# Zeros of a scratch tensor laid by two stages: three channels behind each image's store in attention, two behind each step's store in the scans

## The chip, the cores and the metric

One Trainium2 chip, one core. The metric is the device time of one execution of the whole program in microseconds (us), as the median of several runs. Profiles show one execution each. Engines: PE does matrix products (PEld its weight loads), DVE and ACT elementwise work, POOL (GpSimd) as well, and SP here only issues transfers (DMA).

## The reference

The input x is [32 images, 192 channels, 56, 56] in float32. Four layers follow, each with a group normalisation and a residual:

```
x = x + agent_attention(groupnorm(x))       # layer 0: 6 heads, 49 agents, depthwise 3x3 convolution, projection
x = x + bidirectional_wkv(groupnorm(x))     # layer 1: k, v, r by matrices; scans forwards and backwards over 3136 pixels; layernorm; Wo
x = x + shift_and_blur(groupnorm(x))        # layer 2: each channel shifted by its own offset with zeros beyond the edge, then a 3x3 kernel
x = x + long_convolution(groupnorm(x))      # layer 3: 55x55 filter per channel, by FFT
```

Layers 0 and 1 mix channels within an image. Layers 2 and 3 work on one channel over all images. Layer 2 reads zeros where the shift reaches beyond the image, and that is what the zeros of this change are for.

## The kernel before

The program has four parts in a row: a filter (about the first 190 us), `attention` (layer 0), `scan_pairs` (layer 1), and `channel_blocks` (layers 2 and 3). Between them the data goes through tensors in device memory: `x1` after layer 0, `x2` after layer 1.

**x2 and its gaps.** `x2` is laid out by channel, then half of the images, then row, then image, then column. Rows have a pitch of 112 floats: 56 of data (`x2`) and 56 of zeros (`gaps`). `channel_blocks` reads each channel at an offset in this flat space, so a column beyond the edge reads zeros. The zeros of a channel are one transfer from a small tile `zeros` in on-chip memory: 2 x 57 x 16 pieces of 56 floats (1824 pieces of 224 bytes, 399 KB). There are 192 such transfers, one for each channel; I call one a lay. They write other bytes than the data, and nobody reads them before `channel_blocks`.

**attention.** A loop over 32 images `b`. Two images are in on-chip memory at a time (a pool with two buffers), so the load of image b+2 (L392, L394, in `_Ready.image`) waits for the store of image b (L863, L865). Within an image, four column blocks `j` are worked on:

- `weigh`, `gather` and others on PE, with ACT and DVE between them;
- `convolve`: eight steps on DVE for each of two tiles (L619), the first tap on ACT (L617), from `v_a` and `v_c` that ACT copies out in `find_v` (L593, L604);
- `moments` of the next image: DVE's `bn_stats` on the first tile (L485, seven) and on the second (L487, four), the first use of the loaded image;
- `ask`, `answer`, `project`, and the store.

After each image's store the lays of some channels are issued on SP (L870), six or seven after each of images 0 to 27 and none after the last four. A dependency without a semaphore (`NoSync`) keeps them behind the last store in SP's order.

**scan_pairs.** 16 pairs of images in four chunks of 784 pixels each. It begins by loading weights and constants (L937, L942, L943) and the sums that attention left (L1064, L1066). Then come four `forwards` of the first pair, and a loop of 64 steps. A step interleaves three passes, each of which loads its own three tiles of `x1` (L1019, four transfers on SP):

- `backwards` of a chunk: ACT normalises x (L1111), PE multiplies by Wr (L891, L894, L901, L904 in the helper `_Pairs`), ACT makes the gate g (L1189, L1193, L1194), DVE scans backwards (L1129, L1131), ACT inverts the denominator (L1136, L1137), DVE combines (L1197, L1198, L1199);
- `finish` of the chunk before: PE centres y (weights `fixed`), ACT squares it (L1214), PE takes the mean of the squares, ACT takes the inverse root (L1223, L1224), PE multiplies y by `wog`, DVE scales (L1237) and adds x (L1240), and four stores to `x2` leave on SP (L1254);
- `forwards` of a chunk of the next pair: ACT L1111, PE with Wk and Wv, ACT exp (L1160, `ek`), DVE the product (L1165, `bv`), the scans, y (L1175).

There are seven buffers for the tiles of x, and a load takes three, so a load waits until an earlier pass has let go of its tiles. The last steps of finish are followed by three squares of the new x on ACT (L1247).

The order on each engine's queue is found by a scheduler when the program is built: it lists each engine's instructions by its own estimate of when they become ready. [...] SP's list holds loads, stores and lays together.

Of the kernel before, what the change touches and what calls it, by code (L numbers as in the profile page):

```python
# [28 lines left out]
C = 192  # L29
T = 96  # L30
S = 56
# [38 lines left out]
LEAD = 64  # L70
# [334 lines left out]


@with_exitstack
def attention(ctx: ExitStack, tc: tile.TileContext, a, ready, x1, st_a, st_c, x2, gaps):

# [6 lines left out]
    nc = tc.nc  # L418
    NB = x1.shape[0]
# [15 lines left out]
    n = C + 1  # L435
# [370 lines left out]
    for b in range(NB):  # L806
        x, more = nxt, b + 1 < NB
        if more:
            nxt = ready.image(nc, a, b + 1)
        low, sums = small("low", [PAIR, NK, 3]), small("sums", [PAIR, NK, 3])  # L810
        got = sp.tile([PAIR, NK, C], F32, name="got", tag="got", bufs=1)
        turned, asked, back = {}, {}, {}
        for j in range(NK):
            prs = weigh(j, gk, low, sums)
            if j == 0:
                gq = seen(ag, wqT, gq_c, "gq_a")
            vT = turn_v(j, v[j])
            if j > 0:
                halves = gather(j - 1, *turned[j - 1])
            if j + 2 < NK:  # L820
                v[j + 2] = find_v(j + 2)
            turned[j] = turn(j, prs), vT
            if j > 0:
                settle(j - 1, halves, got)
            if j + 1 < NK:
                o[j + 1] = convolve(j + 1)
            elif more:
                mv, pools = moments(nxt)
        halves = gather(NK - 1, *turned[NK - 1])
        asked[0] = ask(0, gq)  # L830
        settle(NK - 1, halves, got)
        values = join(low, sums, got)
        done, o = o, {}
        st = small("st", [128, 2, 9])
        for t in range(1, NK + 2):
            if t < NK:
                asked[t] = ask(t, gq)
            if more and t == 1:
                mean, d = spread_of(mv)
            if more and t == 2:  # L840
                rs, nb = scaling(mean, d, pools)
                normed(nxt, rs, nb, 0)
            if t <= NK:
                back[t - 1] = turn_back(t - 1, asked[t - 1])
            if more and t in (3, 4):
                v[t - 3] = find_v(t - 3)
            if t >= 2:
                project(t - 2, done[t - 2], x, st)
            if t <= NK:
                answer(t - 1, back[t - 1], values, done[t - 1])  # L850
            if more and t == 2:
                ag = find_agents(b + 1, pools)
                normed(nxt, rs, nb, 1)
            if more and t == 3:
                gk = seen(ag, wkT, gk_c, "gk_a")
                normed(nxt, rs, nb, 2)
            if more and t == 4:
                o[0] = convolve(0)
                normed(nxt, rs, nb, 3)
        nc.sync.dma_start(out=st_a[:, b % 2, b // 2], in_=st[:, 0])  # L860
        for h, r in HALVES:
            nc.sync.dma_start(out=st_c[b % 2, :, h, b // 2], in_=st[r, 1])
        nc.sync.dma_start(out=x1[b, 0:128], in_=x[0].rearrange("p y x -> p (y x)"))  # L863
        for h, r in HALVES:
            stored = nc.sync.dma_start(  # L865
                out=x1[b, 128:C, 1568 * h : 1568 * h + 1568], in_=x[1][r].rearrange("p y x -> p (y x)")
            )
        early = max(1, NB - 4)
        for c in range(C * min(b, early) // early, C * min(b + 1, early) // early):
            laid = nc.sync.dma_start(  # L870
                out=gaps[c].rearrange("s h g w -> (s h) g w"),
                in_=zeros[:, 0:S].unsqueeze(1).to_broadcast([2 * (S + 1), NB // 2, S]),
            )
            behind = mybir.DependencyInfo(mybir.DependencyClass.NoSync, mybir.DependencyReason.DATA)
            tc.add_manual_dep(laid.ins, stored.ins.name, behind, reason="no burst")


class _Pairs:
# [26 lines left out]


@with_exitstack
def scan_pairs(ctx: ExitStack, tc: tile.TileContext, a, k, x1, st_a, st_c, x2, rs2, count):

# [11 lines left out]
    def small(name, shape):  # L923
        return cp.tile(shape, F32, name=name, tag=name)
# [69 lines left out]
    nc.vector.memset(eps, 4.0 * LN_EPS)  # L994
    kept_a, kept_c = small("kept_a", [128, 2, NB // 2]), small("kept_c", [128, NB // 2])
    fine = small("fine", [128, NB // 2])
    tops = small("tops", [128, 5, 3 * NM])
    for i, top in enumerate((1e8, 1e15, 1e15, 1e15, 1e30)):
        nc.vector.memset(tops[:, i], top)
# [202 lines left out]
    def finish(s, m):  # L1202

        h, xs = s.y[m], load(s.p, m)
        hs = [parts(t) for t in h]
        sq = [wp.tile([128, MC], F32, name="sq", tag="t") for _ in range(3)]
        for tiles in ((0, 1), (2,)):
            ps = [turned() for _ in tiles]
            if len(tiles) == 2:
                pairs.outer(centre, [q[2] for q in ps], hs)  # L1210
            else:
                pairs.inner(centre, ps[0][2], hs)
            for t, (_, both, _) in zip(tiles, ps):
                nc.scalar.activation(  # L1214
                    sq[t].rearrange("p (h n) -> p h n", h=2), both, AF.Square,
                    accum_out=s.seen[:, 4, 3 * m + t : 3 * m + t + 1],
                )
        sqs = [parts(t) for t in sq]
        pv = [turned() for _ in range(2)]
        pairs.outer(mean_w, [q[2] for q in pv], sqs)  # L1220
        rds = [wp.tile([128, MC], F32, name="rd", tag="t") for _ in range(3)]
        for t, (_, both, _) in enumerate(pv):
            nc.scalar.activation(rds[t].rearrange("p (h n) -> p h n", h=2), both, AF.Ln, bias=eps)  # L1223
            nc.scalar.activation(rds[t], rds[t], AF.Exp, scale=-0.5)  # L1224

        for t, r in enumerate((slice(0, 64), slice(64, 128))):
            nc.scalar.dma_start(out=rds[2][r], in_=rds[t][r])
        yield
        left = []
        for tiles in ((0, 1), (2,)):  # L1230
            po = [turned() for _ in tiles]
            if len(tiles) == 2:
                pairs.outer(wog, [q[2] for q in po], hs)
            else:
                pairs.inner(wog, po[0][2], hs)
            for t, (_, out, _) in zip(tiles, po):
                nc.vector.tensor_tensor(  # L1237
                    sq[t].rearrange("p (h n) -> p h n", h=2), out, rds[t].rearrange("p (h n) -> p h n", h=2), ALU.mult
                )
                nc.vector.scalar_tensor_tensor(  # L1240
                    xs[t], sq[t], cb[:, of(t)], xs[t], ALU.add, ALU.add, accum_out=s.sums[:, t, m : m + 1]
                )
                if m == NM - 1:
                    nc.vector.tensor_scalar(s.away[:, t], s.sums[:, t, m : m + 1], -1.0 / MC, None, ALU.mult)

                def square(t=t):
                    nc.scalar.activation(  # L1247
                        sq[t], xs[t], AF.Square, bias=s.away[:, t], accum_out=s.squares[:, t, m : m + 1]
                    )

                left.append(square)
        rows = slice(m * MC // S, (m + 1) * MC // S)
        for r, t, i, c in places:
            nc.sync.dma_start(out=x2[c, i, rows, s.p], in_=xs[t][r].rearrange("p (h w) -> p h w", w=S))  # L1254
        yield left

    def conclude(s):
# [546 lines left out]
def all_blocks(ctx: ExitStack, tc: tile.TileContext, a, k, out):  # L1804
# [10 lines left out]
    x2, gaps = wide[..., 0:S], wide[..., S:PITCH]  # L1815
    filt, rs2 = scratch("filt", [C, KS * KS]), scratch("rs2", [C, 2, NB // 2])
    spectra = scratch("spectra", [84, C, 2, 42])
    shifts = scratch("taps", [2 * (S + 1), C // 4, 9]), dp.tile([1, C // 4], I32, name="begins", tag="begins")
    st_a, st_c = scratch("st_a", [128, 2, NB // 2, 9]), scratch("st_c", [2, 64, 2, NB // 2, 9])
    with tc.tile_pool(name="a_r", bufs=1) as rp, tc.tile_pool(name="a_x", bufs=2) as xp:  # L1820
        ready = _Ready(rp, xp)
        make_filter(tc, a, k, filt, spectra, shifts, lambda: ready.load(nc, a, k))
        attention(tc, a, ready, x1, st_a, st_c, flat, gaps)
    with tc.tile_pool(name="count", bufs=1) as cp:
        count = cp.tile([1, 1], I32, name="count", tag="count")
        scan_pairs(tc, a, k, x1, st_a, st_c, x2, rs2, count)
        n = nc.values_load(count[0:1, 0:1], min_val=0, max_val=128)
        with tc.If(n > 0):
            scan_guarded(tc, a, k, x1, x2, rs2)
# [105 lines left out]
```

## Time and profile before

| | us |
|---|---|
| median of 3 runs | 12223.37 (12220.62 to 12237.54) |
| the profiled execution, its own time | 12221.27 |
| its span | 12219.5 |
| attention, about | 190 to 4985 |
| scans, about | 4985 to 8455 |
| channel blocks, about | 8455 to 12219 |
| PE busy | 11048.8 (90%) |
| DVE busy | 10766.9 (88%) |
| ACT busy | 7140.2 (58%) |
| POOL busy | 3332.8 (27%) |
| transfers in SP's queue | 840.69 MB, 30.1% of 16 DMA engines' span |

How to read it: the span is the time from the first to the last event of the profiled execution. "Busy" is an average over three long stages with different limits, so each stage has to be looked at by itself. Times within the profile are counted from the start of the span.

### The profile page before, as it was taken

Reading aid. Unit: us, or ns where it says so; the run is one execution under the profiler, and the core shown is the slowest. Engines: PE = TensorE matmul, PEld = TensorE weight load, DVE = VectorE, ACT = ScalarE, POOL = GpSimd, SP = SyncE. Lnnn points to the kernel's source line nnn. Section 1 sums busy time; section 2 is a strip of 40 time slices with the busy share of each in tenths; the row PEclk is TensorE's granted clock in tenths of the full one; section 3 lists DMA queues with packets and bytes.
Section 4 is the critical chain, followed back from the end, with each engine's and each line's share of the span. In section 5 each row is a group of like instructions: output and inputs, shape, how many; then the busy total and the mean of one; then the engine's idle time right before and its main releaser. Section 6 shows DMA issues by size and latency. Waiting matters only on the chain. (4 is left out here: it accounts for less than half of the span.)

```text
span 12219.5 us, 157479 instructions
## 1 busy us (share of the span) xinstructions
PE 11048.8 (90%) x57358; PEld 6621.1 (54%) x57358; DVE 10766.9 (88%) x14738; ACT 7140.2 (58%) x14684; POOL 3332.8 (27%) x2552
## 2 busy tenths in 40 slices
PE   6999999999999999888888888886999999999999
PEld 3555555555555555433333333333666666666666
DVE  6888888888888888899999999997888898888897
ACT  3555555555555555466666666665666666666665
POOL 0000000000000000365555555554443343343330
PEclk9999999999999999899999999997999999999999
DMA  2222222222222221233433343344332332332331
GB/s 70 58 59 59 58 59 61 59 58 61 64 60 60 60 66 33 64 94 97 104 100 93 100 103 95 96 103 101 72 69 63 68 70 64 67 70 63 67 69 32
DMA packets 1959211, 876.56 MB, mean 72 GB/s; under 512 B 1821153, under 2 KB 1858292, under 8 KB 1949292
## 3 DMA queue, kind: packets, MB, share of 16 engines
q1 hardware_dynamic: 1948188, 840.69, 30.1%
q10 hardware_dynamic: 10240, 25.70, 0.9%
q8 instruction: 458, 7.50, 0.2%
q14 instruction: 325, 2.66, 0.1%
HBM read 482.13 MB, written 319.29 MB: 66 GB/s over the span
## 5 line engine op out<-in xcount | busy, mean ns | idle before, releaser
L619 DVE SCALAR_TENSOR_TENSOR o<-v_a,att_w,o 128x896 f32<-128x896 f32 (+1 forms) x1024 | 1054.6, 1030 | 464.3 <-ACT v_a L593 334.4
L1143 POOL MEMSET f<- 128x1 f32 x96 | 8.9, 99 | 4824.5 <-DMA st_c<-st 4819.5
L1798 ACT COPY y<-ps 64x252 f32<-64x252 f32 (+1 forms) x2376 | 807.9, 340 | 792.2 <-PE ps L1792 761.7
L1631 POOL TENSOR_TENSOR smooth<-smooth,more 114x896 f32<-114x896 f32 x378 | 849.4, 2250 | 1192.0 <-ACT more L1630 1129.2
L1714 PE MATMUL ps<-fixed,real 84*84 84x112 f32 x6144 | 1092.1, 259 | 0.0
L1714 PE MATMUL ps<-fixed,imag 84*84 84x112 f32 x6144 | 1090.2, 259 | 0.0
L1722 ACT ACTIVATE z<-ps,rs 84x112 f32<-84x112 f32 x3072 | 817.4, 355 | 324.5 <-PE ps L1714 322.1
L1714 PEld LDWEIGHTS ps<-fixed,real 84*84 84x84 f32 x6144 | 789.1, 153 | 158.5 <-issue 128.9
L1136 ACT ACTIVATE q<-q 128x784 f32<-128x784 f32 x384 | 328.3, 855 | 805.9 <-DVE q L1131 636.4
L1714 PEld LDWEIGHTS ps<-fixed,imag 84*84 84x84 f32 x6144 | 764.6, 153 | 0.0
L636 ACT ACTIVATE pr<-ps,low 98x896 f32<-98x896 f32 (+1 forms) x384 | 352.1, 917 | 592.5 <-DVE low L634 592.5
L891 PE MATMUL ps<-sq,fixed 128*128 128x392 f32 x512 | 299.1, 747 | 425.9 <-ACT sq L1214 425.9
L724 PE MATMUL ps<-gq_a,xs_a 128*112 128x294 f32 x1792 | 626.1, 431 | 44.0 <-DVE pq L729 44.0
L1792 PE MATMUL ps<-fixed,padded 114*128 114x168 f32 x3072 | 525.4, 320 | 132.1 <-DVE x L1734 115.3
L619 DVE SCALAR_TENSOR_TENSOR o<-v_c,att_w,o 128x448 f32<-128x448 f32 (+1 forms) x1024 | 635.6, 621 | 6.0 <-ACT v_c L604 0.9
L632 PE MATMUL ps<-xs_a,gk_a 128*98 128x448 f32 (+1 forms) x1536 | 637.1, 495 | 0.0
L633 PE MATMUL ps<-xs_c,gk_c 125*98 125x448 f32 (+1 forms) x1536 | 631.6, 492 | 0.0
L725 PE MATMUL ps<-gq_c,xs_c 125*112 125x294 f32 x1792 | 611.5, 423 | 0.0
L1733 PE MATMUL ps<-z,fixed 84*114 84x448 f32 x1536 | 609.9, 539 | 1.0 <-ACT z L1722 1.0
L891 PE MATMUL ps<-x,weights 128*128 128x392 f32 x1536 | 572.3, 515 | 30.5 <-DVE bv L1165 15.9
L737 ACT ACTIVATE pq<-pq 112x1176 f32<-112x1176 f32 x224 | 265.3, 1184 | 571.8 <-DVE pq L729 449.0
L1792 PEld LDWEIGHTS ps<-fixed,padded 114*128 114x128 f32 x3072 | 469.8, 196 | 205.5 <-DVE x L1734 139.5
(376 smaller groups left out, 29202.2 us busy)
## 6 DMA issues: line engine op xcount, KB each, us to landing
x<-x SPq DMA_DIRECT2D x576, 392.0 KB
x<-x SPq DMA_DIRECT2D x512, 196.0 KB
x<-zeros SPq DMA_DIRECT2D x192, 399.0 KB
shifted<-x SPq DMA_DIRECT2D x192, 399.0 KB
x<-x SPq DMA_DIRECT2D x192, 399.0 KB
out_x<-x SPq DMA_DIRECT2D x384, 196.0 KB
x<-in_x SPq DMA_DIRECT2D x32, 1568.0 KB
x<-x SPq DMA_DIRECT2D x32, 1568.0 KB
```

The source lines that it names most:

```text
L619: nc.vector.scalar_tensor_tensor(dst, tap(i), dww[:, t, i : i + 1], dst, ALU.mult, ALU.add)
L632: mm(ps[P2, h, :n], g[:, cols], xs_a[j][:, px], start=True, stop=False)
L633: mm(ps[P2, h, :n], gk_c[0:KC, 2 * j + h, cols], xs_c[j][0:KC, px], start=False, stop=True)
L724: mm(ps[:SUB, i, :HA], xs_a[j][:, px], g, start=True, stop=False)
L725: mm(ps[:SUB, i, :HA], xs_c[j][0:KC, px], gq_c[0:KC, 2 * j + (q + i) // ns], start=False, stop=True)
L891: mm(out, aa, srcs[t][h], start=True, stop=False)
L1631: nc.gpsimd.tensor_tensor(y, y, more, ALU.add)
L1714: nc.tensor.matmul(ps[:84, i * 2 * S : (i + 1) * 2 * S], part[:, i0 + i].rearrange("p s u -> p (s u)"), f3[:, m, :], start=(m == 0), stop= ...
L1722: nc.scalar.activation(z[:, i0 + i].rearrange("p m w -> p (m w)"), ps[:84, i * 2 * S : (i + 1) * 2 * S], AF.Copy, scale=q.rs[:, i0 + i : i ...
L1733: nc.tensor.matmul(got, f4[:, m, :], z[:, i0 : i0 + n, m, :], start=(m == 0), stop=(m == 1))
L1792: nc.tensor.matmul(ps[:, g * 168 : (g + 1) * 168], flat[:, (g0 + g) * 128 : (g0 + g + 1) * 128], f1, start=True, stop=True)
L1798: nc.scalar.copy(y[64 * m : 64 * m + 64, 2 * g0 + i : 2 * (g0 + n) : 2], got[64 * i : 64 * i + 64, :, :, m, :])
```

## The change

Both stages get a helper `lay(behind, zeros, n)`. It takes the next `n` channels of a list `bare` that have no zeros yet, and issues their lays on SP behind the given store. `tc.issue_after` sets the same kind of dependency as before: order of issue only, with no wait for the store to finish. Attention calls it with 3 after each of its 32 images. The scans get a `zeros` tile of their own, filled once by POOL, and call it with 2 after each step's stores (in the last pair with all that is left, which is nothing, as the list is empty after 48 steps).

```diff
-def attention(ctx: ExitStack, tc: tile.TileContext, a, ready, x1, st_a, st_c, x2, gaps):
+def attention(ctx: ExitStack, tc: tile.TileContext, a, ready, x1, st_a, st_c, x2, lay):
...
-        early = max(1, NB - 4)
-        for c in range(C * min(b, early) // early, C * min(b + 1, early) // early):
-            laid = nc.sync.dma_start(
-                out=gaps[c].rearrange("s h g w -> (s h) g w"),
-                in_=zeros[:, 0:S].unsqueeze(1).to_broadcast([2 * (S + 1), NB // 2, S]),
-            )
-            behind = mybir.DependencyInfo(mybir.DependencyClass.NoSync, mybir.DependencyReason.DATA)
-            tc.add_manual_dep(laid.ins, stored.ins.name, behind, reason="no burst")
+        lay(stored, zeros, 3)
...
-def scan_pairs(ctx: ExitStack, tc: tile.TileContext, a, k, x1, st_a, st_c, x2, rs2, count):
+def scan_pairs(ctx: ExitStack, tc: tile.TileContext, a, k, x1, st_a, st_c, x2, rs2, count, lay):
...
+    zeros = small("zeros", [2 * (S + 1), LEAD])
+    nc.gpsimd.memset(zeros, 0.0)
...
-            nc.sync.dma_start(out=x2[c, i, rows, s.p], in_=xs[t][r].rearrange("p (h w) -> p h w", w=S))
+            stored = nc.sync.dma_start(out=x2[c, i, rows, s.p], in_=xs[t][r].rearrange("p (h w) -> p h w", w=S))
+        lay(stored, zeros, 2 if s.p + 1 < NP else C)
...
+    bare = list(range(C))
+
+    def lay(behind, zeros, n):
+
+        with tc.issue_after(behind.ins):
+            for c in bare[:n]:
+                nc.sync.dma_start(
+                    out=gaps[c].rearrange("s h g w -> (s h) g w"),
+                    in_=zeros[:, 0:S].unsqueeze(1).to_broadcast([2 * (S + 1), NB // 2, S]),
+                )
+        del bare[:n]
...
-        attention(tc, a, ready, x1, st_a, st_c, flat, gaps)
+        attention(tc, a, ready, x1, st_a, st_c, flat, lay)
...
-        scan_pairs(tc, a, k, x1, st_a, st_c, x2, rs2, count)
+        scan_pairs(tc, a, k, x1, st_a, st_c, x2, rs2, count, lay)
```

In the changed program the lays have line L1820, and most lines of the scans lie five lower than before (L1019 is L1014 there, L1111 is L1106, L1240 is L1235).

## The prediction

> **What bounds the kernel now.** I read the busy rows of the 40 slices first, then the same by stage.
>
> ```profile
> PE   6999999999999999888888888886999999999999
> DVE  6888888888888888899999999997888898888897
> DMA  2222222222222221233433343344332332332331
> 190.00:4985.00 4795.00, 4528.12 (x25748) 2763.82 (x25744) 4059.15 (x6134) 2580.97 (x4616) 0.64 (x20) 0.98 0.26 56
> 5150.00:8455.00 3305.00, 2746.70 (x10054) 1256.07 (x10052) 3187.69 (x3320) 2102.63 (x3613) 1859.66 (x1624) 0.92 0.40 99
> ```
>
> The last two rows are attention and the scans: length, then busy us of PE, PEld, DVE, ACT and POOL, granted clock, DMA share, GB/s. Attention is PE's (4528 of 4795), with DVE in turn; the scans are DVE's (3188 of 3305, 96%). DMA is far from full in both, so bytes cost nothing here; what counts is what a store or a load stands behind. All zeros and nearly all loads go through SP, in one order. So next: what one lay of zeros takes there, and who waits behind it.
>
> ```profile
> L870 SPq DMA_DIRECT2D x<-zeros x192: 1268/5769/6543, 355.2 to 4441.9; - x192
> 954.48 36.57 SPq L870 DMA_DIRECT2D x<-zeros  x7
> 991.09 6.20 SPq L392 DMA_DIRECT2D x<-in_x  x1
> 1005.52 1.15 DVE L485 BATCH_NORM_STATS2 st_a<-x 128x6 f32<-128x448 f32 x2 [1.77 <-DMA x<-in_x]
> DVE st_a L485 <- DMA x<-in_x: 37.4, 24, 3.1
> 4733.50 1.67 DVE L485 BATCH_NORM_STATS2 st_a<-x 128x6 f32<-128x448 f32 x3
> ```
>
> A lay holds the queue 5.77 us. Seven hold the next image's load back 37 us, and DVE waits for it 37.4 us in 24 images (rows of the waits: us in total, times, longest). The last row is an image with no lays ahead of its load.
>
> Then one step of the scans, where the new lays go:
>
> ```profile
> 6134.29 6.93 SPq L1254 DMA_DIRECT2D x<-x  x4
> 6141.32 41.22 SPq L1019 DMA_DIRECT2D x<-x  x12
> 6147.87 1.02 ACT L1111 ACTIVATE x<-x,nb,rs 128x784 f32<-128x784 f32 x1
> 6148.25 2.90 PE L891 MATMUL ps<-x,weights 128*128 128x392 f32 x8
> 6170.00 5.59 PE L891 MATMUL ps<-sq,fixed 128*128 128x392 f32 x8 [8.82 <-ACT sq L1214]
> 6184.54 0.97 DVE L1237 TENSOR_TENSOR sq<-ps,rd 128x784 f32<-128x784 f32 x1 [1.66 <-PE ps L894]
> ACT x L1111 <- DMA x<-x: 9.8, 16, 2.1
> ```
>
> The store's four DMAs go out; right behind them the last two tiles of the backward x (L1019). By the landing events the first lands at 6147.6, and ACT normalises it at 6147.87: 0.3 us to spare. Over the steps that I followed so, that spare time is 0.3 to 3.6 us; the stores are 53.1 us apart in the mean. Waits are small (last row) only because the loads come just in time.
>
> **What the skill says.** "DMA: Bandwidth & Descriptors", section "Queues, rings and completion order": SP has one ring on each of the DMA engines, and descriptors are consumed in ring order. The trace agrees: seven lays move the load by seven lays. "TensorE: Matmul & The Clock Gate", section "What's actually happening": after an idle window of about 3.4 us the array runs at half rate, and it takes some 3.4 us of work to release it. The trace agrees: after the 8.82 us wait above, eight matmuls take 5.59 us, those at 6148.25 take 2.90; the scans' clock is 0.92.
>
> **Part 1, attention: three lays behind each of 32 images, where six or seven stood behind 28.** I count from the issue of the image's store (L863). With seven lays, DVE's first L485 on the next image starts at +56.5 (median), on the landing. Four lays fewer, 4 x 5.77, put it at +33.4. But the built order of the changed program also moves three of seven L485 some 35 instructions forward, as in the images without lays, where they start at +31.1 (4733.50 less 4702.36). So DVE still waits, 2.3 us. That wait covers one of 1.5 us for ACT v_a (L593) that now stands at this place. Two ways to sum: (a) by waits, seven lays cost 1.5 + 37.4/24 = 3.1 us, six lays 1.5, no lays 0, three 2.3: 24 x -0.8 + 4 x 0.8 + 2 x 2.3 = -11 us. (b) by spacing of the stores: 150.55 (seven), 148.4 (six), 146.8 (none; two images), so 149.1 for three: 24 x -1.45 + 4 x 0.7 + 2 x 2.3 = -27. I take **-18**; the ends are -96 (all images like those without lays) and +15.
>
> **Part 2, the seam.** Now three lays also follow the last image's store, ahead of every constant and load of the scans. DMA is 0.97 busy from 4985 to 5000, and PE waits 10.43 us for the first of these loads (L956). Nothing covers it: 3 x 5.77 = **+17**. The zeros' memset on POOL is one more of 0.16 us (L460), while POOL waits for loads anyway: nothing.
>
> **Part 3, the scans: two lays behind each of 48 stores** (96 channels left), none in the last 16 steps. They are 11.5 us that L1019 stands behind. In the step shown, the tile lands at 6159.1 instead of 6147.6, the next one 1.3 later. The built order answers: ACT's third ek (L1160) now stands ahead of these two L1111, and DVE does more scanning before it asks for L1197. What is queued behind: on PE, the rest of the r matmul, then the matmuls on y (L891 to L904, fixed); on ACT, L1136, two g (L1189) and the squares (L1214). Followed with the durations of the step:
>
> - ACT L1111 end at 6160.2 and 6161.5; q's inverse (L1136, L1137) 6163.3; DVE wants it at 6163.84: just hidden.
> - PE, at full clock: r's second part 6161.7, first y 6163.2, r's rest 6164.8, the remaining y (1.5 + 1.6 + 3.1) 6171.0.
> - ACT: two g with their logarithms and exponentials among two inverses and three squares, 0.8 to 1.0 each, end with the third square at 6176.6; before 6171.4.
> - PE: the mean over squares ends 6178.3 (6177.1 before, slow clock); L1223 and L1224 on ACT, PE on wog: 6185.1, and DVE L1237 starts at 6185.2 instead of 6184.54: +0.7 us.
> - But PE now idles from 6149.7 to 6160.2, over 10 us, ahead of that chain instead of ahead of the mean, so the chain starts at half clock. The gap in the trace cost 5.59 - 2.90 = 2.7; I take 2.0, as some falls where PE waits again.
>
> From the step's last x (L1240) the store goes out, and the next delay is counted from there: a loop store, lays, load, r, squares, mean, wog, x. It now lasts 53.1 + 2.7 = 55.8 us, longer than DVE's 53.1 a step. DVE becomes the one that waits, at L1237 and after. 48 x 2.7 = **+130**. The ends: 0 (the loop fits under DVE) and 5 us a step, +240 (full slow clock, and the inverses late as well). A gain in this stage is excluded: nothing there is removed, and no load comes sooner.
>
> The channel stage keeps its order on every engine: nothing.
>
> **Sum:** -18 + 17 + 130 = +129. The profiled execution took 12221.3 (span 12219.5), 2.1 under the median of the three, 12223.4. So 12350 for such an execution, **12352** as a median.
>
> **Rivals.**
>
> 1. *The scans hide it (0.18).* If two lays cost at most some 9 us ahead of the load, or the array stays warm, the loop stays within 53.1 and DVE hides it all. For it: scan stores with the same 224-byte packets drain faster, four within some 10 us; PE has 8.8 us of idle later in the step to give. Against: 5.77 was measured on the same instruction with the same shape, and the idle PE time is used in the sum. Time: 12223 - 18 + 17 = 12222, not slower; with the whole attention gain, 12223 - 96 + 17 = 12144.
> 2. *DVE stalls twice a step (0.17).* If ACT's L1111 comes 2 us later than I have it, L1136 behind it misses DVE's 6163.84, and the cold clock costs 2.7: 5 us a step, 12223 + 240 = 12462.
> 3. *The change is not what it says (0.03).* The lays could have been built ahead of loads or elsewhere; the built order shows 32 x 3 and 48 x 2 behind their stores, so no.
>
> The forecast case has 0.62, with its own range 12280 to 12410.
>
> **Chances.** 0.2% is 24 us, about what a measurement of this kernel can tell from no change. Rival 1 falls on both sides of -24, mostly within; the low end of the forecast case adds a little to "same". Slower 0.79, same 0.12, faster 0.09. Range 12215 to 12435, which leaves out half of rival 2 and the best of rival 1.
>
> **What would show it.** Right: lays of 5.8 us at L1820, 32 x 3 and 48 x 2; in the scans ACT L1111 waits on DMA x for some 10 us in each laid step, PE's wait moves from the squares to the r matmul, DVE waits more at L1237, steps of 55 to 56 us up to the twelfth pair and 53 after; L485 still waits in attention; scans begin some 17 us later relative to the last store. Wrong: steps of 53 with lays, or L485 without waits and store spacing near 147.

## The result, and the profile after

The change makes the kernel slightly faster: 12204.28 us median (12189.79 to 12217.05, 13 runs) against 12228.05 us (12215.89 to 12262.48, 13 runs) for the kernel before in the same session; ratio 0.9979, 95% interval 0.997 to 0.9987. The forecast was 12352, slower, with 12215 as the low end. It was wrong in sign and the time fell outside the range.

First the same rows of the page and of the windows as before the change: the busy tenths of PE and DVE, then attention, the seam and the scans (length; busy us of PE, PEld, DVE, ACT, POOL; granted clock; DMA share; GB/s).

```profile
PE   6999999999999999788888888886999999999999
DVE  6888888888888888799999999997889898898897
190.00:4985.00 4795.00, 4538.82 (x25880) 2787.37 (x25880) 4077.90 (x6201) 2596.89 (x4644) 10.03 (x39) 0.98 0.20 50
4985.00:5150.00 165.00, 128.40 (x404) 54.78 (x400) 161.05 (x144) 86.74 (x148) 101.86 (x89) 0.86 0.25 64
5150.00:8455.00 3305.00, 2733.90 (x9951) 1242.98 (x9950) 3139.07 (x3275) 2076.75 (x3573) 1936.84 (x1614) 0.92 0.51 110
```

The windows are fixed in time, so the first now reaches past attention into the scans: the stage has become shorter. In the scans the DMA share went from 0.40 to 0.51 and DVE's busy time fell from 3188 to 3139 us in the same length, so DVE waits more (the third window also reaches some 10 us past the end of the scans now); the clock is 0.92 in both.

To see where time went I mark the same instructions in both traces: each image's store in attention, the first normalised x of the scans (ACT's activation x<-x,nb,rs), each step's store, and, for the length of a step, its third x (DVE's x<-sq,cb,x, L1235 now).

| stretch of the profiled execution | before | after | difference |
|---|---|---|---|
| start to the first image's store | 349.7 | 346.8 | -2.9 |
| first to last image's store | 4628.8 | 4562.3 | -66.5 |
| mean spacing of the stores of images 1 to 29 | 150.09 | 147.68 | |
| last image's store to the first normalised x of the scans | 32.3 | 49.0 | +16.7 |
| first normalised x to the first step's store | 165.3 | 166.8 | +1.5 |
| first step's store to the 49th | 2559.8 | 2602.1 | +42.3 |
| mean step of these, without the first | 53.36 | 54.07 | +0.71 |
| 49th step's store to the last | 711.0 | 708.5 | -2.5 |
| last step's store to the first store of the output | 152.5 | 151.1 | -1.4 |
| first to last store of the output | 3615.2 | 3616.6 | +1.4 |
| whole span | 12219.5 | 12208.0 | -11.5 |

The two profiled executions are 11.5 us apart, the medians 24; the stages are read from the profiled pair. Attention gives 66.5, the seam (from the last image's store to the first normalised x) takes 16.7 back and the laid steps 42.3. Of these, 9.3 lie in the first step, and each of the 47 that follow is longer by 0.71 in the mean. Two early ones took about 58 us each; from the fifth on the difference is 0.54. The remaining rows come to -4 together.

DVE's waits in attention (us in total, times, longest) and PE's at the seam show the first two:

```profile
DVE st_a L485 <- DMA x<-in_x: 31.4, 30, 2.4
4936.47 2.29 PE L949 MATMUL ps<-passing 128*128 128x1 f32 x12 [27.05 <-DMA passing<-in_scan_c]
```

DVE waits for the next image in 30 images instead of 24, 1.0 us each instead of 1.6. PE's first wait in the scans grew from 10.43 to 27.05 us, by 16.6, for the three lays that now stand ahead of these loads.

Then one laid step of the scans, first SP, ACT and PE by the timeline (start, duration, what is done; in brackets the idle time ahead and what ended it):

```profile
6110.04 6.06 SPq L1249 DMA_DIRECT2D x<-x  x4
6116.14 5.84 SPq L1820 DMA_DIRECT2D x<-zeros  x2
6122.09 35.60 SPq L1014 DMA_DIRECT2D x<-x  x12
...
6133.06 1.04 ACT L1106 ACTIVATE x<-x,nb,rs 128x784 f32<-128x784 f32 x1 [9.47 <-DMA x<-x]
...
6134.16 2.98 PE L884 MATMUL ps<-x,weights 128*128 128x392 f32 x4 [8.79 <-ACT x L1106]
6136.93 2.70 PE L884 MATMUL ps<-y,fixed 128*128 128x392 f32 x4
...
6141.08 1.58 PE L884 MATMUL ps<-y,fixed 128*128 128x392 f32 x4
...
6148.32 3.13 PE L884 MATMUL ps<-sq,fixed 128*128 128x392 f32 x8 [1.15 <-ACT sq L1209]
...
6160.40 1.86 DVE L1232 TENSOR_TENSOR sq<-ps,rd 128x784 f32<-128x784 f32 x2 [2.68 <-PE ps L887]
```

The mechanism is the one forecast. The store goes out, two lays follow, the load waits behind them, ACT waits 9.47 us for it and PE 8.79 us for ACT. PE's long wait has moved from the squares to the r matmul, and the slow clock has moved with it: four matmuls take 2.98 us and the next four 2.70, where four of the same shape take 1.58 a little later; the eight on the squares are back to 3.13 from 5.59. Between 5200 and 8400 the waits (us in total, times, longest) say the same:

```profile
ACT x L1106 <- DMA x<-x: 479.8, 103, 10.1
PE ps L884 <- ACT x L1106: 366.2, 47, 9.5
```

And yet the step is 54.1 us long, not 55.8. The experiments ask what a lay costs at each place, and which of the three terms was mis-sized.

### The profile page after: what moved, and what is told of

The parts are those of the page before. It is cut to its first block, busy times and chain, and to the rows that moved or that the text cites. A ratio compares the mean times of both kernels' runs of the same rounds, so it can differ in the third digit from the quotient of the medians.

```text
span 12208.0 us, 157529 instructions
## 1 busy us (share of the span) xinstructions
PE 11045.0 (90%) x57358; PEld 6628.8 (54%) x57358; DVE 10751.6 (88%) x14738; ACT 7133.8 (58%) x14684; POOL 3443.0 (28%) x2553
## 5 line engine op out<-in xcount | busy, mean ns | idle before, releaser
L884 PE MATMUL ps<-x,weights 128*128 128x392 f32 x1536 | 652.7, 567 | 393.9 <-ACT x L1106 368.5
L884 PEld LDWEIGHTS ps<-x,weights 128*128 128x128 f32 x1536 | 300.7, 210 | 693.4 <-ACT x L1106 405.9
L1106 ACT ACTIVATE x<-x,nb,rs 128x784 f32<-128x784 f32 x384 | 389.5, 1033 | 490.6 <-DMA x<-x 490.1
```

The source lines that it names most:

```text
L884: mm(out, aa, srcs[t][h], start=True, stop=False)
```

## The experiments

**The theories.** A: only the place in the queue counts. A lay costs what it delays the load behind it, less what the waiting engine has to spare, so a lay that no load waits behind is free. B, the rival: the bytes cost as well, 399 KB a lay (409 thousand bytes), wherever the lay stands. Ratios below are to the kernel before, run on the same chip; its median there lay between 12224 and 12231 us. Steps, spacings and seams are read from one trace of each kernel by the marks of the table above.

In several kernels a step's load carries lays behind its first tile instead, where ACT and DVE are still busy with earlier work and nothing waits for the next load yet. I call that place the slot. Its code, the same in all of them:

```diff
-    def load(p, m):
+    def load(p, m, n=0):
...
-            nc.sync.dma_start(out=xs[t][r], in_=ap)
+            loaded = nc.sync.dma_start(out=xs[t][r], in_=ap)
+            if t == 0:
+                lay(loaded, zeros, n)
...
-    def normed(s, m):
-        xs = load(s.p, m)
+    def normed(s, m, n=0):
+        xs = load(s.p, m, n)
```

### The two lays of a step, moved to the slot

Attention is as in the change.

```diff
-        xn = normed(s, m)
+        xn = normed(s, m, 2 if s.p > 0 else 0)
...
-        lay(stored, zeros, 2 if s.p + 1 < NP else C)
```

> Attention as in the change; in the scans the two lays of a step stand behind the first tile of the forward load, where SP goes on to wait some 29 us for PE, instead of behind the step's stores. Theory A (what is queued behind a lay decides): the backward load lands in time again, ACT's 10 us waits on it vanish, steps return from 54.07 to about 53.4 us, so some 33 us less than the changed kernel: 12171. Theory B (the extra bytes in this stage cost time wherever they stand): steps stay at 54.1, time 12204.

Measured: 12168.5 us (12154.08 to 12184.63), ratio 0.9952 (0.9938 to 0.9965). Steps 53.33 us, spacing of the image stores 147.88, seam 48.9. The same bytes, moved past a load's first tile, cost nothing in a step, so the +0.71 is the place and not the bytes: theory A. With the lays gone from behind the store the built order of PE, DVE and ACT in the steps is again that of the kernel before; in the change it is another. So the place stands here for two things, the delay of the load and the order that the scheduler built around it, and the +0.71 is not divided between them.

### The last image's three lays left to the scans

```diff
-        lay(stored, zeros, 3)
+        lay(stored, zeros, 3 if more else 0)
```

> As the change, but no lays behind the last image; its three channels are laid in the scans, in two more steps. Theory A: the constants and loads of the scans no longer stand behind 17 us of lays, which nothing covers: about 17 less than the changed kernel, one of it given back by the later steps: 12188. Rival (the seam is bound by something else, and the lays were only in front of a wait that is there anyway): 12204.

Measured: 12187.82 us (12184.04 to 12191.2), ratio 0.9966 (0.9954 to 0.9978). The seam is 32.4 us, as in the kernel before, with steps of 54.03 and the built order of the change. So the three lays after the last image cost 16.6 us, where the forecast had 17 for them.

### No lay in attention, three behind each step's store

```diff
-        lay(stored, zeros, 3)
...
-        lay(stored, zeros, 2 if s.p + 1 < NP else C)
+        lay(stored, zeros, 3)
```

> No lays in attention; three behind the stores of all 64 steps of the scans. Theory A: the loop store, lays, load, gate, squares, mean, x grows by one lay, 5.8 us a step, to about 59.9 us, as it is now just longer than DVE's own step: 64 x 6.5 = 420 more than before in the scans, 96 less in attention, no seam: about 12550. Theory B: the cost of a lay in the scans is that of its bytes, 0.7 / 2 us each: 64 x 3 x 0.35 = 67 more, less 96: about 12200.

Measured: 12531.68 us (12529.57 to 12542.12), ratio 1.0249 (1.0235 to 1.0263). Steps 59.66; image spacing 146.75; seam 32.5. One of PE's groups between 5200 and 8300 (busy us, mean ns, then idle time ahead and its causes), and the row of that window, with columns as in the first block:

```profile
L883 PE MATMUL ps<-x,weights 128*128 128x392 f32 x1242 | 545.7, 579 | 770.9 <-ACT x L1105 756.8 <-DVE sq L1231 13.7 <-DVE bv L1159 0.5
5200.00:8300.00 3100.00, 2320.38 (x8470) 1047.46 (x8468) 2717.33 (x2781) 1779.50 (x3041) 1395.12 (x1404) 0.86 0.54 109
```

DVE's busy time falls to 2717 of 3100 us and the clock to 0.86: the loop of store, lays, load and r now sets the step. One more lay than in the change costs 59.66 - 54.07 = 5.59 us a step, nearly all of its 5.77. This is what the forecast had feared for two lays; it comes true at the third. The built order of ACT differs here too, so part of the 5.59 may be order.

### All 192 lays in the slot, none in attention

```diff
-        lay(stored, zeros, 3)
...
-        xn = normed(s, m)
+        xn = normed(s, m, 0 if s.p == 0 else 4 if s.p < 4 else 3)
...
-        lay(stored, zeros, 2 if s.p + 1 < NP else C)
```

> No lays in attention; three or four behind the first tile of the forward load in each of the 60 steps that have one. Theory A: 17 to 23 us of lays fit the 29 us in which SP waits for PE there, so nothing waits for them: steps 53.4, no seam, attention as in the images without lays (146.8 us an image): 12228 - 96 = about 12132, or some 10 more if the last lay runs past the wait. Theory B: 12200.

Measured: 12124.29 us (12121.89 to 12131.01), ratio 0.9916 (0.9903 to 0.993). Steps 53.41, image spacing 146.75, seam 32.2, and in the steps the built order of the kernel before. So all 192 lays cost the kernel before about 103 us (0.84%), and in the slot they cost nothing that the steps show.

### The number of lays behind an image: two, four and five

The rest goes to the slot of the scans. Only the counts differ; for two lays:

```diff
-        lay(stored, zeros, 3)
+        lay(stored, zeros, 2)
...
-        xn = normed(s, m)
+        xn = normed(s, m, 3 if s.p > 0 else 0)
```

> Two lays behind each image, the other 128 in the free place of the scans; three L485 early. Theory A: the load lands at +26.4, ahead of DVE's +31.2, so attention runs as without lays (146.75) and only the seam is left, 11.5: 12136. Rival (DMA traffic during attention costs by itself): spacing 147.3, 12153.

Four lays, two in the slot:

> Four lays behind each image in attention, the other 64 in the free place of the scans. The built order again has three L485 early, as with three lays. Theory A: the image's load lands 5.8 us later than with three, at +38.0, and DVE, which wants it at +31.2, waits 6.8 us: store spacing 146.75 + 6.8 = 153.5, 30 images, seam +23: 12124 + 204 + 23 = 12351. Rival (fewer lays are better by themselves, the place of L485 matters little): spacing about 148.2, 12124 + 44 + 23 = 12191.

Five lays, one in the slot:

> Five lays behind each image, the other 32 in the free place of the scans. Here the built order has all seven L485 late, as with seven lays before. Theory A: the load lands at about +44, DVE wants it at +55 and does not wait; only the 1.5 us for ACT v_a stay open: spacing about 148.4, 30 x 1.65 + seam 29: 12124 + 79 = 12203, so five lays are faster than four. Rival (fewer lays are better): spacing 149 or more, and slower than four lays.

| lays behind an image | time, us | ratio (interval) | spacing | seam | step |
|---|---|---|---|---|---|
| 2 | 12132.61 | 0.9926 (0.9912 to 0.994) | 146.75 | 43.1 | 53.39 |
| 3 (the first experiment) | 12168.5 | 0.9952 (0.9938 to 0.9965) | 147.88 | 48.9 | 53.33 |
| 4 | 12387.61 | 1.0135 (1.012 to 1.0151) | 154.75 | 54.9 | 53.37 |
| 5 | 12202.12 | 0.9981 (0.9975 to 0.9988) | 148.25 | 60.5 | 53.38 |

The waits of DVE's L485 with four lays, beside the 31.4 us of three:

```profile
DVE st_a L485 <- DMA x<-in_x: 217.1, 30, 8.1
```

Five lays are faster than four by 185 us. The built order explains it: up to four lays three of the seven L485 stand early. In the images that I compared, the orders of PE, DVE and ACT are the same with two, three and four lays, and the three L485 are nearly all that moves with five. With two lays the first of them starts at +31.1 us from the image's store without a wait (the medians), with three at +32.1 and with four at +38.4, both on the landing of the load: DVE waits 0, 1.0 and 217.1/30 = 7.2 us. With five lays the scheduler puts all seven late, at +55.1, and the wait is gone. The spacing follows: with four lays 8.0 us above two. That is more than the wait alone, and it is why four lays took some 37 us more than was expected of them. The seam grows by 5.6 to 6.0 us with each lay.

### One lay behind each step's store, the other 128 in the slot

```diff
-        lay(stored, zeros, 3)
...
-        xn = normed(s, m)
+        xn = normed(s, m, 0 if s.p == 0 else 3 if s.p < 3 else 2)
...
-        lay(stored, zeros, 2 if s.p + 1 < NP else C)
+        lay(stored, zeros, 1)
```

> No lays in attention; one behind the stores of each of the 64 steps, the other 128 behind the first tile of the forward load (where lays cost nothing). Theory A, a loop against a threshold: with two lays the loop takes 54.07 us, with three 59.66, so with one 48.4, below DVE's own 53.4, and the step stays at 53.4: time as with none behind the stores, 12124. Rival (each lay behind the stores costs a third of 6.3, evenly): steps 55.5, 12124 + 64 x 2.1 = 12258.

Measured: 12097.14 us (12090.09 to 12103.62), ratio 0.9896 (0.9881 to 0.9911). It is the fastest kernel of the study, and no theory had it: with one lay ahead of the load the steps are shorter, 52.70 instead of 53.41. (The interval overlaps a little with that of all lays in the slot; the steps are read from one trace of each.) PE's matmuls on the squares, of r and on y between 5200 and 8000, DVE's wait for the scaling between 5200 and 8400, then the window 5200 to 8300, first with all lays in the slot and then with one behind the store:

```profile
L883 PE MATMUL ps<-sq,fixed 128*128 128x392 f32 x424 | 257.8, 773 | 385.3 <-ACT sq L1210 385.3
L883 PE MATMUL ps<-x,weights 128*128 128x392 f32 x1248 | 452.6, 505 | 0.0
L883 PE MATMUL ps<-y,fixed 128*128 128x392 f32 x420 | 160.7, 515 | 55.5 <-DVE bv L1161 55.5
DVE sq L1233 <- PE ps L886: 72.7, 43, 9.1
5200.00:8300.00 3100.00, 2571.62 (x9441) 1175.93 (x9442) 3012.15 (x3116) 1977.54 (x3394) 1766.78 (x1544) 0.93 0.56 122
```

```profile
L883 PE MATMUL ps<-sq,fixed 128*128 128x392 f32 x424 | 186.3, 566 | 129.8 <-ACT sq L1210 129.8
L883 PE MATMUL ps<-x,weights 128*128 128x392 f32 x1280 | 530.0, 545 | 178.6 <-ACT x L1107 174.1 <-DVE sq L1233 4.5
L883 PE MATMUL ps<-y,fixed 128*128 128x392 f32 x426 | 199.7, 592 | 61.3 <-DVE mean L1034 28.5 <-DVE rs L1045 23.7 <-DVE bv L1161 9.1
DVE sq L1233 <- PE ps L886: 20.6, 6, 8.9
5200.00:8300.00 3100.00, 2662.60 (x9586) 1177.29 (x9585) 3036.81 (x3151) 2004.26 (x3446) 1829.94 (x1551) 0.95 0.60 124
```

PE waits less at one place and more at another: 385.3 us at the squares became 129.8 there and 174.1 at the r matmul. The slow matmuls moved with the waits: those on the squares went from 773 to 566 ns, while those of r (in one group with k and v) went from 505 to 545 and those on y from 515 to 592. One step, by the timeline:

```profile
6047.55 2.98 PE L883 MATMUL ps<-x,weights 128*128 128x392 f32 x4 [3.60 <-ACT x L1107]
6050.33 2.82 PE L883 MATMUL ps<-y,fixed 128*128 128x392 f32 x4
6064.57 1.58 PE L883 MATMUL ps<-sq,fixed 128*128 128x392 f32 x4 [2.19 <-ACT sq L1210]
```

After a wait of 3.60 us four matmuls take 2.98 us, after one of 2.19 they take 1.58. The Trainium skill, "TensorE: Matmul & The Clock Gate", section "What's actually happening", has the half rate follow from an idle window of about 3.4 us; this step agrees. But slow matmuls did not become fewer: between 5200 and 8000, 473 matmuls of 392 columns took over 650 ns, where 363 did with all lays in the slot. The higher granted clock, 0.95 instead of 0.93, counts PE's idle time as well: the half rate was granted for 271 us here and 416 there, but PE was at work in 254 us of it here and in 230 there.

What changed is where the half-rate matmuls stand: ahead of ACT's squares, and no longer between the squares and x. In the mean of 47 steps the third square ends 33.1 us after the last x of the step before, where it was 32.8, but from there to the first matmul of wog it takes 4.8 us instead of 7.3, and DVE's scaling (L1233) starts at +43.6 instead of +44.8. DVE hardly waits for it any more: 6 times between 5200 and 8400 instead of 43. The kernels with two and three lays save the same 2.4 to 2.6 us behind the squares, measured against the kernel before, but there the squares end 3.7 and 8.6 us later, so the scaling stands at +45.7 and +50.8. That is how one lay can go with a gain, and two or three with a loss.

The built order differs between none and one lay as well, with the work of ACT, DVE and PE interleaved otherwise, so whether the delay moved the squares' wait or the order did is not separated here. The next run was meant to.

### A short copy in the place of that lay

Behind each store stands a copy of about as many bytes in long rows. It was meant to keep the order that the scheduler builds, while the queue is free again sooner.

```diff
+    spare = scratch("spare", [32, S, S])
...
-        xn = normed(s, m, 0 if s.p == 0 else 3 if s.p < 3 else 2)
+        xn = normed(s, m, 0 if s.p == 0 else 4 if s.p < 4 else 3)
...
-        lay(stored, zeros, 1)
+        lay(stored, a["x"][0, 0:32], 0)
...
+            if n == 0 and len(zeros.shape) == 3:
+                nc.sync.dma_start(out=spare, in_=zeros)
```

> The kernel with one lay behind each store of the scans, changed in one thing: behind the store stands a copy of 401 KB from an input to a scratch array that nothing reads, in 12544-byte rows, in place of the lay of 409 KB in 224-byte pieces; all 192 lays stand in the free slot (four in the first five pairs' steps, three later). The scheduler sees nearly the same bytes there, so the built order of PE, DVE and ACT stays nearly that of that kernel, while the copy should go through the queue in some 2 to 3 us, worked out from bytes, not 5.8. If the order made the steps 52.7 us long instead of 53.4, they stay at 52.7 and the time is near 12097, PE's wait for the squares notwithstanding. If the delay made them so, by splitting PE's long idle stretch, most of it goes: steps 53.1 to 53.4, wait on the squares' matmul back to over 250 us and its mean near 770 ns between 5200 and 8000, time 12115 to 12130.

Measured: 12188.84 us (12184.25 to 12202.01), ratio 0.9968 (0.9957 to 0.9979). Steps 54.33: longer than in both outcomes that were expected. PE's matmuls on the squares and the window in this kernel, read as above:

```profile
L883 PE MATMUL ps<-sq,fixed 128*128 128x392 f32 x416 | 246.4, 740 | 198.6 <-ACT sq L1210 198.6
5200.00:8300.00 3100.00, 2624.29 (x9294) 1172.32 (x9292) 2963.43 (x3052) 1946.69 (x3341) 1814.95 (x1528) 0.92 0.58 128
```

The order did not stay. On ACT it is another one in every step: ahead of the first square stand six instructions of q's inversion in the kernel with one lay, and seven or eight here, and ahead of such instructions ACT idles 15.5 us a step up to the third square, instead of 10.0. The third square ends 35.3 us after the last x, against 33.1 there and 32.8 with all lays in the slot, and 700 matmuls took over 650 ns, against 473 and 363. So this run does not take delay and order apart. It shows a step 0.92 us longer than with all lays in the slot, though the load is hardly held back: the first normalised x starts at +9.0 here, at +8.2 with all lays in the slot and at +12.2 with the one lay (medians). Whether the one lay's gain comes from its delay, or from the order that the scheduler built around it, stays open. (The channel stage was 15 us longer as well in this execution, which no theory has; the steps are what counts here.)

## Why the prediction was wrong

**The seam (+17): right.** Measured +16.7, and the run without them took it away.

**The scans (+130): wrong in size.** Measured +0.71 us a step, 42 in all with the first. The steps of the sum, in us from the last x of the step before (L1240, done at 6139.75 before; L1235, done at 6114.62 in the step shown):

| | forecast, at full clock | measured in the step shown |
|---|---|---|
| normalised x starts (ACT L1106) | +19.35 | +18.4 |
| first g on ACT (L1184), behind the last matmul of r | +25.15 | +26.5 |
| third square on ACT ends | +36.85 | +36.7 |
| DVE L1232 starts | +45.45 | +45.8 |
| and with 2.0 for the slow clock | +47.45 | |

This instruction stood at +44.8 before (L1237 there), so the forecast had it 2.65 us later; it came 1.0 later in the step shown, and in the mean of 47 steps as well, 45.7 instead of 44.7. The slow clock was priced well: 2.98 + 2.70 us where full rate takes 2 x 1.58, so 2.5 us in place of the 2.0 that I took. The step that failed is the chain to which I added it: it was too long. I had the tile land 0.9 us late: the two lays delayed the normalised x by 10.3 us, where I had 2 x 5.77. And from the first g to the end of the third square I had 11.7 us, for thirteen activations that I had put at 0.8 to 1.0 each; the trace shows 10.2. They last 10.9 us together, so 0.8 of the difference is durations taken too long, and 0.7 is overlap, which I left out:

```profile
6144.28 0.85 ACT L1189 ACTIVATE g<-g 128x784 f32<-128x784 f32 x1
6145.03 0.85 ACT L1131 ACTIVATE q<-q 128x784 f32<-128x784 f32 x1
6145.77 0.85 ACT L1189 ACTIVATE g<-g 128x784 f32<-128x784 f32 x1
```

Each lasts 0.85 us, and the next starts after 0.75. The Trainium skill has the overlap, in "ScalarE: Activation LUTs", section "What ACT_TABLE_LOAD costs": back-to-back activations overlap by about 93 ns. The trace agrees (0.10). With the slow clock at 2.3 us between normalised x and first g, and 0.45 us more than forecast behind the squares, the sum is 0.65 + 2.3 - 0.9 - 1.5 + 0.45 = 1.0. The step grows by less, 0.71, since from L1232 to the third x it now takes 8.4 us and took 8.7 (means).

The forecast's rule was right, a loop that outgrows DVE's own work sets the step, and the run with three lays shows it. What it missed is that DVE already waited for this loop before the change. The waits between 5200 and 8400, before and after:

```profile
DVE sq L1237 <- PE ps L894: 55.7, 42, 2.1
DVE sq L1232 <- PE ps L887: 95.9, 52, 3.2
```

So the old step, 53.36 us in the mean and not 53.1, was no floor set by DVE alone, and it was wrong to exclude a gain in this stage: in the kernel with one lay nothing was removed and no load came sooner, and yet its steps are 52.70, with the slow matmuls no longer behind the squares. Rival 1 came nearest, though by neither of its two conditions: the lays did hold the load back by some 10 us, and the array did go slow. I gave it 0.18, and its scans did not stay as they were either.

**Attention (-18): mis-sized.** Measured -66.5. The place of L485 was right, three early, and DVE does wait. The term that failed is the wait that stays: 1.0 us and not 2.3, since the image lands at +32.2 rather than +33.4. Four lays fewer brought it 24.3 us forward, 6.1 a lay and not 5.77. With 1.0 in place of 2.3, sum (b) has a spacing of 146.8 + 1.0 = 147.8, against 147.68 measured, and comes to 24 x -2.75 - 4 x 0.6 + 2 x 1.0 = -66 instead of -27. So 39 of the missing 48 us are this one wait, counted in 30 images, and the other 9 came from averaging (b) with (a). Sum (a) counts only what DVE loses at this one instruction, while the spacing of the stores also holds what waits for DVE later: with the right wait (a) would have said -50. The run with four lays shows the same from the other side: 7.2 us of wait cost 8.0 of spacing.

**The sum.** Neither error alone made the sign: with 42 for the scans the forecast's sum is +41, with -66 for attention +81, and only with both -7. The channel stage kept its length within 1.4 us. With the measured terms the sum is 12221.3 - 66.5 + 16.7 + 42.3 = 12213.8 for the profiled execution, 12209.75 in fact; the -4 is that of the table. That lies between the two values that I gave for rival 1, 12222 and 12144, but by other terms than its own. The low end of the range, 12215, cut off the part of rival 1 in which attention gains more than 25.

## What to carry to other kernels

A transfer that nothing waits for still costs what the load behind it in the queue can't spare: put it behind the first part of a load that is needed late, where 192 lays of 5.8 us cost nothing here that the steps show. When following a chain through one engine, take the distance from start to start of its instructions, not the sum of durations. Look whether the engine that seems to set the pace already waits for the chain: then a change of the chain shows in both directions. When a stage's period can be read for the state that you expect, use the period rather than the waits at one instruction, and ask how much the result hangs on a small remainder, as here on a wait of 1.0 or 2.3 us in 30 images. And look at the cliffs: one lay behind a step's store went with a gain of 0.7 us, two cost 0.7, a third 5.6 more, and four behind an image more than five.

## What was not expected of the hardware

With one lay of 5.8 us ahead of a load that PE is about to need, a step took 52.70 us instead of 53.41, although more matmuls ran slow, 473 over 650 ns instead of 363. What a slow matmul costs depends here on what stands behind it: with such matmuls moved from behind the squares to ahead of them, the way from the third square to wog was 2.5 us shorter, and the third square ended only 0.3 us later. The delay or the built order that came with it may have moved them; the runs do not say which. A higher mean clock was no sign of faster work either: 0.95 instead of 0.93, with more of PE's busy time at half rate.

The other surprise was in the built order: between four and five lays the scheduler moved three instructions of DVE in each image, and 185 us of time with them.
